# Graph network, layer 2: where x and its constants are added, and how the second norm gets its variance

## The chip, the cores and the metric

The kernel runs on one core of a Trainium2 chip. The metric is the time of one execution on the device in microseconds. A core has five engines with a queue each: TensorE (PE, its weight loads PEld), VectorE (DVE), ScalarE (ACT), GpSimd (POOL) and SyncE (SP). SP only issues DMAs here. GpSimd issues the indirect DMAs (gathers and scatters by a list of row numbers). Sixteen DMA engines carry all of them.

## The reference

A two-layer graph attention network over 10,000 nodes with 768 features and 170,000 edges (self loops included), and a residual norm around it. Cut to what matters:

```python
h = gat_conv(x, edge_index, W1, a_src1, a_dst1, b1, HEADS, HID, True)     # 4 heads of 256
h = relu(layer_norm(h, g1, be1)) + (x @ Wr1 + br1)
h1 = h                                                                   # 1024 columns
h = gat_conv(h, edge_index, W2, a_src2, a_dst2, b2, 1, OUT_DIM, False)   # 1 head of 768
h = layer_norm(h, g2, be2)
h = h + (h1 @ Wr2 + br2)
return _layernorm(x + h)                                                 # no gain, no bias
```

Each `gat_conv` takes, for every node, the softmax over its incoming edges and sums the source nodes' rows by it, and adds its bias. So the end of layer 2 is, for each node: a weighted sum of gathered rows plus b2, a first norm with g2 and be2, the addition of h1 @ Wr2 + br2 and of x, and a second norm. All numbers are float32.

## The kernel before

**Tiles and slots.** Nodes are sorted by their degree and cut into 79 tiles of 128, one node on each partition. A tile of n slots fetches n rows for each of its 128 nodes: slot 0 is the tile's own rows (a plain DMA from SP, L452), the other n - 1 are gathers on GpSimd (L424, one for each slot, 128 rows of 770 numbers). `TURNS` puts the tiles in the order in which both layers work: every other one from small degrees to large, then the rest back. So n runs 8, 10, 11, 12 and so on up to 41 in the middle (tile 39 in this order) and down again to 9; it is 15 to 19 in about half of the tiles, and 1377 in all. Layer 1 (up to about 3428 us) writes each tile's 1024 columns to `h1_d`, its x rows to `x_d` and the rows that layer 2 gathers to `table2`.

**Layer 2** (`ordered_layer2`, L878 on) keeps a ring of 41 slots in SBUF. `ring.fetch(q)` (L449) issues the fetches up to q. The fetch of a slot waits until the slot 41 before it has been read, by VectorE and by TensorE.

For a tile t, in the program's order:

- `residual(t)` (L942), issued a tile ahead on TensorE: into PSUM it sums x (by a product with the identity matrix, L949) and h1 @ Wr2 (L952), 768 columns in two parts.
- `weights_of(t)` (L923), issued inside tile t - 1: its first part, at slot `turn` of that tile (a third of the way, later where the ring is tight), makes the logits of all n slots on VectorE (L477 to L484) and their exponential on ScalarE. It needs all rows of tile t. Its second part, three slots later, makes the weights on VectorE (L496 to L499), on ScalarE a diagonal matrix for each slot (L937), and on TensorE the weighted sum of the last 256 columns (L938), behind the residual in the same PSUM tile.
- The loop over the n slots: VectorE adds each slot's first 512 columns, times its weight, to `acc` in PSUM (`weigh`, L519). Its first addition takes b2 in place of `acc`, so that one reads two tiles in SBUF, ring and b2; the others read one in SBUF and one in PSUM. After each slot, `ring.fetch` goes on by one (L1002). At slot n // 2 the loads of h1 and x for tile t + 2 are issued on SP (`fetch_x`, L903 and L904).
- `norms(t)` (L957), a generator that runs on inside tile t + 1. Step 1, before that tile's first slot: mean and variance of the weighted sum by VectorE's statistics (L577, L579), Ln and Exp on ScalarE (L581, L582). Step 2, at slot 3: `scaled` (L591 twice, L593: times g2 and the deviation, plus be2, which also holds br2 and the share of br1), the addition of the PSUM residual (L962), and mean and variance of the result (L577 twice, L579, then L581 and L582 again). Step 3, at slot 6: minus mean times deviation (L966, VectorE) and the output on ScalarE (L968). Step 4, at slot 9: the scatter to `out` on GpSimd (L970).

Each engine takes its instructions in the program's order, which is written by hand. Two addresses matter: x of the first two tiles is loaded into the end of the ring, for later tiles into parts of the space of W2, which layer 2 doesn't need any more.

The lines that set the order:

```python
if k in (turn, turn + LEAD):            # LEAD is 3
    ready += itertools.islice(ahead, 1)  # weights_of(t + 1)
if k in (LEAD, 2 * LEAD, 3 * LEAD):
    next(last, None)                     # norms(t - 1), steps 2, 3, 4
weigh(acc, ring.slot(FIRST[t] + k), e[:, k], ON_PE2, None if k else b2_b)
ring.fetch(FIRST[t] + k + 1 + ring.size)
if t + 2 < NT and k == n // 2:
    ins[t + 2] = fetch_x(t + 2)
```

Of the kernel before, what the change touches and what calls it, by code (L numbers as in the profile page):

```python
# [28 lines left out]
F32 = mybir.dt.float32  # L29
# [6 lines left out]
P = 128  # L36
# [43 lines left out]
def gnn_kernel(ctx, tc, x, x_cols, src, dst, src_col, dst_col, W1, a_src1, a_dst1, b1, g1, be1, Wr1, br1,  # L80
# [492 lines left out]
    def deviation(small, parts):  # L573

        st = small.tile([P, len(parts), 6], F32, name="st")
        for j, a in enumerate(parts):
            nc.vector.bn_stats(st[:, j, :], a)  # L577
        mv = small.tile([P, 2], F32, name="mv")
        nc.vector.bn_aggr(mv, st.rearrange("p k s -> p (k s)"))  # L579
        sd = small.tile([P, 1], F32, name="sd")  # L580
        nc.scalar.activation(sd, mv[:, 1:2], AF.Ln, bias=eps)  # L581
        nc.scalar.activation(sd, sd, AF.Exp, scale=-0.5)  # L582
        return mv[:, 0:1], sd
# [294 lines left out]
    def ordered_layer2():  # L878
        nonlocal ps_big
        with tc.tile_pool(name="b2", bufs=1) as pool, tc.tile_pool(name="small2", bufs=2) as small, \  # L880
# [17 lines left out]
            firsts = [(at_end(C1), at_end(D0)) for _ in range(min(2, NT))][::-1]  # L898

            def fetch_x(t):  # L900

                hT, xt = firsts[t] if t < 2 else (parts[t % 2], parts[2 + t % 2][:, :D0])
                nc.sync.dma_start(hT, h1_d[t])  # L903
                nc.sync.dma_start(xt, x_d[t])  # L904
                return hT.rearrange("p (k n) -> p k n", n=P), xt

            ins = {0: fetch_x(0)}
            ring.fetch(SLOTS[0])
            adds = [spread(pool, shift, "out", nc.sync)]
            b2_b = spread(pool, b2, "b2", nc.sync)  # L910
            ins[1] = fetch_x(1)
            g2_b, be2_b = (spread(pool, v, n, nc.sync) for v, n in ((g2, "g2"), (be2, "be2")))
            nc.vector.tensor_add(b2_b, b2_b, adds[0][:, :C2])
            adds.append(spread(pool, br2, "out", nc.sync))
            assert SLOTS[0] <= rest // R2 and NT > 1

            ones = pool.tile([1, P], F32, name="ones")
# [24 lines left out]
            def residual(t):  # L942


                hT, xt = ins.pop(t)
                r = ps_big.tile([P, 2 * BANK], F32, name="big")
                for c in range(0, C2, BANK):
                    d = min(C2, c + BANK)
                    nc.tensor.matmul(r[:, c:d], ident, xt[:, c:d], start=True, stop=False,  # L949
                                     skip_group_check=True)  # L950
                    for j in range(K1):
                        nc.tensor.matmul(r[:, c:d], hT[:, j, :], wr2[:, j, c:d], start=False,  # L952
                                         stop=(j == K1 - 1 and d < C2),
                                         skip_group_check=True)
                return r

            def norms(t, h, r, means):  # L957

                stats = deviation(small, [a for m in means for a in pieces(m, C2 - ON_PE2)])
                yield  # L960
                scaled(h, means, stats, g2_b, be2_b)
                nc.vector.tensor_add(h, h, r[:, :C2])  # L962
                mean, inv = deviation(small, pieces(h, C2 // 2))
                yield
                less = small.tile([P, 1], F32, name="less")
                nc.vector.scalar_tensor_tensor(less, mean, -1.0, inv, op0=OP.mult, op1=OP.mult)  # L966
                o = pool.tile([P, C2], F32, name="out")
                nc.scalar.activation(o, h, AF.Identity, bias=less, scale=inv)  # L968
                yield
                nc.gpsimd.indirect_dma_start(  # L970
                    out=out, out_offset=bass.IndirectOffsetOnAxis(ap=nodes(t), axis=0),
                    in_=o, in_offset=None, bounds_check=N - 1, oob_is_err=False)
# [7 lines left out]
            for t in range(NT):  # L980
# [15 lines left out]
                for k in range(n):  # L996
                    if k in (turn, turn + LEAD):
                        ready += itertools.islice(ahead, 1)
                    if k in (LEAD, 2 * LEAD, 3 * LEAD):
                        next(last, None)  # L1000
                    weigh(acc, ring.slot(FIRST[t] + k), e[:, k], ON_PE2, None if k else b2_b)
                    ring.fetch(FIRST[t] + k + 1 + ring.size)  # L1002
                    if t + 2 < NT and k == n // 2:
                        ins[t + 2] = fetch_x(t + 2)
                ready += ahead
                for _ in last:
                    pass
# [2 lines left out]
                    nc.vector.tensor_add(be2_b, be2_b, q[:, :C2])  # L1010
                last = norms(t, h, rs[t], [acc, rs[t][:, C2:2 * C2 - ON_PE2]])
                if t + 2 < NT and t + 2 not in ins:
                    ins[t + 2] = fetch_x(t + 2)
            for _ in last:
                pass

# [269 lines left out]
```

## Time and profile before

| | us |
|---|---|
| median of 6 runs | 5322.07 (5316.48 to 5326.01) |
| the profiled execution | 5326.81 |
| its span | 5325.0 |
| busy in the span: PE, DVE, POOL, ACT | 4762.9, 4284.2, 3230.5, 2798.2 |
| layer 2: its first gather, its last gather, its last scatter | 3428.30, 5255.52, 5312.86 |

The profile's second part cuts the span into 40 slices of 133 us, with the busy share in tenths. Layer 2 is the last 14 or so:

```profile
PE   8999997999999986678999999999998866889998
DVE  5884244899999888788899999589988766789998
ACT  3433443677777776677887777333333222233332
POOL 3445455555666655656666655277777656777774
PEclk9999998999999988889999999999998887889999
DMA  4333625899999998799999999599999989999995
```

A reader should keep in mind that shares are means over a slice, that matmuls are pipelined and their ends modelled, and that instructions which only issue a DMA from SP or wait are not counted as busy. In a timeline, a row is: start, length, engine, line, operation, what it writes and reads, how many are merged, and in brackets the idle time before it with what ended that. In a table of groups, the columns are the count, the busy us with the mean ns of one, and the idle us before them.

### The profile page before, as it was taken

How to read it: one execution, taken by the hardware profiler on the slowest of the kernel's cores; microseconds unless marked ns; L12 is line 12 of the kernel's file. 1: busy time of each engine (PE TensorE's matmuls, PEld its weight loads, DVE VectorE, ACT ScalarE, POOL GpSimd, SP SyncE). 2: the span in 40 equal slices, each digit the busy share in tenths (PEclk: the TensorE clock that was granted, in tenths of full speed). 3: DMA queues.
4: the chain of work that ended last, by engine and by line, in shares of the span. 5: the costliest groups of instructions: out<-in, count | busy, mean ns of one | idle time of the engine just before them, and what ended most of it. 6: DMA issues, size and time to landing. Idle time of an engine off the chain costs nothing. (4 is left out here: it accounts for less than half of the span.)

```text
span 5325.0 us, 59568 instructions
## 1 busy us (share of the span) xinstructions
PE 4762.9 (89%) x15191; PEld 2860.2 (54%) x15191; DVE 4284.2 (80%) x7729; ACT 2798.2 (53%) x8184; POOL 3230.5 (61%) x3159
## 2 busy tenths in 40 slices
PE   8999997999999986678999999999998866889998
PEld 3444443555555554445555555566666544566665
DVE  5884244899999888788899999589988766789998
ACT  3433443677777776677887777333333222233332
POOL 3445455555666655656666655277777656777774
PEclk9999998999999988889999999999998887889999
DMA  4333625899999998799999999599999989999995
GB/s 157 123 100 87 97 87 188 317 335 346 354 368 362 366 332 298 270 330 346 359 365 364 351 333 334 186 381 377 379 366 347 327 275 321 331 352 371 367 384 219
DMA packets 474306, 1591.37 MB, mean 299 GB/s; under 512 B 118327, under 2 KB 122487, under 8 KB 473958
## 3 DMA queue, kind: packets, MB, share of 16 engines
q0 software_dynamic: 322384, 1286.62, 66.2%
q1 hardware_dynamic: 149520, 297.43, 16.2%
q10 hardware_dynamic: 2054, 3.42, 0.2%
q8 instruction: 128, 2.10, 0.2%
q14 instruction: 220, 1.80, 0.1%
HBM read 1431.80 MB, written 177.29 MB: 302 GB/s over the span
## 5 line engine op out<-in xcount | busy, mean ns | idle before, releaser
L424 POOL DMA_INDIRECT ring<-table,slots x2675 | 2649.9, 991 | 1498.4 <-DVE acc L519 373.8
L519 DVE SCALAR_TENSOR_TENSOR acc<-ring,e,acc 128x512 f32<-128x512 f32 (+1 forms) x2530 | 1578.2, 624 | 123.1 <-PE acc L733 47.5
L508 ACT ACTIVATE ring<-ring,e 128x256 f32<-128x256 f32 x3284 | 1337.7, 508 | 0.0
L515 DVE TENSOR_TENSOR acc<-acc,ring 128x1024 f32<-128x1024 f32 x801 | 985.6, 1230 | 79.8 <-ACT ring L508 11.0
L938 PE MATMUL big<-ring,diagonals 128*128 128x256 f32 x2754 | 684.6, 411 | 196.1 <-ACT diagonals L937 186.3
L171 PE MATMUL big<-w,xT 128*128 128x512 f32 x1896 | 827.7, 599 | 22.5 <-DMA w<-in_W_dram 9.9
L826 PE MATMUL half<-w,hT 128*128 128x512 f32 (+1 forms) x2528 | 830.5, 486 | 0.0
L171 PE MATMUL big<-wr,xT 128*128 128x512 f32 x1896 | 830.1, 595 | 0.2 <-ACT xT L706 0.2
L952 PE MATMUL big<-wr,w 128*128 128x512 f32 (+1 forms) x2464 | 822.8, 487 | 0.0
L938 PEld LDWEIGHTS big<-ring,diagonals 128*128 128x128 f32 x2754 | 564.2, 207 | 313.7 <-ACT diagonals L937 217.0
L826 PEld LDWEIGHTS half<-w,hT 128*128 128x128 f32 x2528 | 478.9, 189 | 371.2 <-issue 308.9
L733 PE MATMUL acc<-ring,diagonals 128*128 128x256 f32 x1912 | 481.2, 410 | 193.4 <-ACT diagonals L727 193.0
L952 PEld LDWEIGHTS big<-wr,w 128*128 128x128 f32 x2464 | 470.6, 191 | 327.8 <-issue 296.6
L171 PEld LDWEIGHTS big<-w,xT 128*128 128x128 f32 x1896 | 364.0, 193 | 482.2 <-issue 464.5
L171 PEld LDWEIGHTS big<-wr,xT 128*128 128x128 f32 x1896 | 356.5, 191 | 417.4 <-issue 416.7
L733 PEld LDWEIGHTS acc<-ring,diagonals 128*128 128x128 f32 x1912 | 389.5, 207 | 278.0 <-ACT diagonals L727 217.3
L581 ACT ACTIVATE sd<-mv,eps 128x1 f32<-128x1 f32 x237 | 69.6, 294 | 814.2 <-DVE mv L579 814.2
L937 ACT ACTIVATE diagonals<-ident,e 128x128 f32<-128x128 f32 x1377 | 410.9, 387 | 140.6 <-DVE e L499 131.6
L665 DVE TENSOR_TENSOR scr<-big,ad_b 128x1024 f32<-128x1024 f32 x79 | 96.7, 1224 | 377.9 <-ACT row L662 377.9
L727 ACT ACTIVATE diagonals<-ident,e 128x128 f32<-128x128 f32 x956 | 293.0, 388 | 204.0 <-DVE e L499 203.9
L485 ACT ACTIVATE e<-e 128x68 f32<-128x68 f32 (+29 forms) x160 | 38.2, 239 | 635.9 <-DVE e L484 635.9
L670 POOL TENSOR_TENSOR row<-row,none 128x1024 f32<-128x1024 f32 x79 | 187.1, 2368 | 264.5 <-ACT row L662 264.0
(173 smaller groups left out, 3617.4 us busy)
## 6 DMA issues: line engine op xcount, KB each, us to landing
ring<-table,slots POOLq DMA_INDIRECT x2675, 7.0
table<-row SPq DMA_DIRECT2D x79, 516.0 KB, 3.6
h_d<-hT SPq DMA_DIRECT2D x79, 512.0 KB, 6.5
w<-h_d SPq DMA_DIRECT2D x77, 512.0 KB, 8.3
table<-row SPq DMA_DIRECT2D x79, 385.0 KB, 6.0
ring<-table SPq DMA_DIRECT2D x79, 385.0 KB, 6.5
xT<-in_x_cols_dram SPq DMA_DIRECT2D x79, 384.0 KB, 4.5
x_d<-xt SPq DMA_DIRECT2D x79, 384.0 KB, 6.6
```

The costliest lines, as they stand in the source:

```text
L171: nc.tensor.matmul(p[:, c:e], aT[:, j, :], w[:, j, c:e], start=(j == 0), stop=(j == k - 1))
L424: nc.gpsimd.indirect_dma_start(out=to, out_offset=None, in_=table, in_offset=bass.IndirectOffsetOnAxis(ap=index, axis=0), **more)
L508: nc.scalar.activation(row[:, s], row[:, s], AF.Copy, scale=e[:, h:h + 1])
L515: nc.vector.tensor_add(acc[:, :c], acc[:, :c], row[:, :c])
L519: nc.vector.scalar_tensor_tensor(acc[:, s], row[:, s], e[:, h:h + 1], (acc if first is None else first)[:, s], op0=OP.mult, op1=OP.add)
L670: nc.gpsimd.tensor_add(row[:, :C1], row[:, :C1], b1_b)
L727: nc.scalar.activation(diagonals[:, k * H1 + i, :], ident, AF.Copy, scale=e[:, k, i:i + 1])
L733: nc.tensor.matmul(acc[:, c:d], diagonals[:, k * H1 + i, :], ring.slot(q + k)[:, c:d], start=(k == 0 and c % BANK == 0), stop=(k == m - 1 ...
L826: nc.tensor.matmul(q, hT[:, j, :], w2[:, j, c:c + q.shape[1]], start=(j == 0), stop=(j == K1 - 1))
L937: nc.scalar.activation(diagonals[:, k % G, :], ident, AF.Copy, scale=e[:, k, :])
L938: nc.tensor.matmul(to, diagonals[:, k % G, :], ring.slot(FIRST[t] + k)[:, ON_PE2:C2], start=False, stop=(k == n - 1), skip_group_check=True)
L952: nc.tensor.matmul(r[:, c:d], hT[:, j, :], wr2[:, j, c:d], start=False, stop=(j == K1 - 1 and d < C2), skip_group_check=True)
```

## The change

It touches layer 2 only.

- x is no longer summed by TensorE. `residual` starts with the h1 product. x is loaded into two fixed places (`xs`, in W2's space) by a load of its own.
- In step 1 of `norms`, after the statistics, VectorE adds `be2_b` to x in place. In step 2, `scaled` adds this sum where it added `be2_b`.
- The addition of the PSUM residual becomes a form that also gives the sum of each row (`total`). VectorE's statistics of the result (L577 twice, L579) and L966 go.
- In step 3, ScalarE makes minus the mean from that sum, squares the centred row with the sum of squares as a second output (the squares land in `o` and are overwritten), takes Ln and Exp for the deviation, and makes the output.
- The load of x for tile t + 2 is issued after step 2 of `norms(t)`, so inside tile t + 1 at slot 3; h1's stays at slot n // 2 of tile t. At the start of the layer, x of tiles 0 and 1 is loaded after the first ring rows and constants, and no longer into the ring.

```diff
+            firsts = [at_end(C1) for _ in range(min(2, NT))][::-1]
+            xs = [parts[2 + i][:, :D0] for i in range(2)]
+
+            def fetch_h(t):
+
+                hT = firsts[t] if t < 2 else parts[t % 2]
+                nc.sync.dma_start(hT, h1_d[t])
+                return hT.rearrange("p (k n) -> p k n", n=P)
 
             def fetch_x(t):
-
-                hT, xt = firsts[t] if t < 2 else (parts[t % 2], parts[2 + t % 2][:, :D0])
-                nc.sync.dma_start(hT, h1_d[t])
-                nc.sync.dma_start(xt, x_d[t])
-                return hT.rearrange("p (k n) -> p k n", n=P), xt
-
-            ins = {0: fetch_x(0)}
+                nc.sync.dma_start(xs[t % 2], x_d[t])
+
+            ins = {0: fetch_h(0)}
             ring.fetch(SLOTS[0])
             adds = [spread(pool, shift, "out", nc.sync)]
             b2_b = spread(pool, b2, "b2", nc.sync)
-            ins[1] = fetch_x(1)
+            ins[1] = fetch_h(1)
+            fetch_x(0)
             g2_b, be2_b = (spread(pool, v, n, nc.sync) for v, n in ((g2, "g2"), (be2, "be2")))
             nc.vector.tensor_add(b2_b, b2_b, adds[0][:, :C2])
             adds.append(spread(pool, br2, "out", nc.sync))
+            if NT > 1:
+                fetch_x(1)
...
             def residual(t):
-                hT, xt = ins.pop(t)
+                hT = ins.pop(t)
...
-                    nc.tensor.matmul(r[:, c:d], ident, xt[:, c:d], start=True, stop=False,
-                                     skip_group_check=True)
                     for j in range(K1):
-                        nc.tensor.matmul(r[:, c:d], hT[:, j, :], wr2[:, j, c:d], start=False,
+                        nc.tensor.matmul(r[:, c:d], hT[:, j, :], wr2[:, j, c:d], start=(j == 0),
...
             def norms(t, h, r, means):
 
                 stats = deviation(small, [a for m in means for a in pieces(m, C2 - ON_PE2)])
+                nc.vector.tensor_add(xs[t % 2], xs[t % 2], be2_b)
                 yield
-                scaled(h, means, stats, g2_b, be2_b)
-                nc.vector.tensor_add(h, h, r[:, :C2])
-                mean, inv = deviation(small, pieces(h, C2 // 2))
+                scaled(h, means, stats, g2_b, xs[t % 2])
+                total = small.tile([P, 1], F32, name="all")
+                nc.vector.scalar_tensor_tensor(h, r[:, :C2], 1.0, h, op0=OP.mult, op1=OP.add, accum_out=total)
+                if t + 2 < NT:
+                    fetch_x(t + 2)
                 yield
+                o = pool.tile([P, C2], F32, name="out")
                 less = small.tile([P, 1], F32, name="less")
-                nc.vector.scalar_tensor_tensor(less, mean, -1.0, inv, op0=OP.mult, op1=OP.mult)
-                o = pool.tile([P, C2], F32, name="out")
-                nc.scalar.activation(o, h, AF.Identity, bias=less, scale=inv)
+                nc.scalar.activation(less, total, AF.Copy, scale=-1.0 / C2)
+                nc.scalar.activation(o, h, AF.Square, bias=less, accum_out=total)
+                nc.scalar.activation(total, total, AF.Ln, bias=eps, scale=1.0 / C2)
+                nc.scalar.activation(total, total, AF.Exp, scale=-0.5)
+                nc.scalar.activation(less, less, AF.Copy, scale=total)
+                nc.scalar.activation(o, h, AF.Identity, bias=less, scale=total)
                 yield
...
                     if t + 2 < NT and k == n // 2:
-                        ins[t + 2] = fetch_x(t + 2)
+                        ins[t + 2] = fetch_h(t + 2)
```

More of the change, by code (lines that the diff above doesn't have):

```diff
@@ L897, in ordered_layer2 @@
             nc.vector.tensor_copy(brT, br1_c[:, :, None].to_broadcast([P, K1, P]))
-            firsts = [(at_end(C1), at_end(D0)) for _ in range(min(2, NT))][::-1]
-            def fetch_x(t):
-                hT, xt = firsts[t] if t < 2 else (parts[t % 2], parts[2 + t % 2][:, :D0])
-                nc.sync.dma_start(hT, h1_d[t])
-                nc.sync.dma_start(xt, x_d[t])
-                return hT.rearrange("p (k n) -> p k n", n=P), xt
-            ins = {0: fetch_x(0)}
+            firsts = [at_end(C1) for _ in range(min(2, NT))][::-1]
[4 more added lines that the diff above has]
+                return hT.rearrange("p (k n) -> p k n", n=P)
+            def fetch_x(t):
+                nc.sync.dma_start(xs[t % 2], x_d[t])
+            ins = {0: fetch_h(0)}
             ring.fetch(SLOTS[0])
@@ L1012, in ordered_layer2 @@
                 if t + 2 < NT and t + 2 not in ins:
-                    ins[t + 2] = fetch_x(t + 2)
+                    ins[t + 2] = fetch_h(t + 2)
             for _ in last:
```

## The prediction

> **What bounds the kernel now.** Layer 2 runs from 3428 us to 5313 us; nothing before it changes. The chain of waits was read first and says nothing here: it holds only the last output scatter. So I took the busy times in four stretches of layer 2 (length; then busy us and instructions of PE, PEld, DVE, ACT, POOL; clock, DMA share, GB/s):
>
> ```profile
> 3440.00:4050.00 610.00, 589.89 (x2081) 397.33 (x2080) 537.61 (x1106) 200.47 (x635) 456.01 (x472) 0.98 0.99 374
> 4050.00:4750.00 700.00, 532.06 (x1808) 374.30 (x1807) 520.09 (x983) 195.24 (x626) 473.08 (x496) 0.85 0.90 320
> 4750.00:5256.00 506.00, 487.69 (x1716) 329.40 (x1716) 471.14 (x958) 169.03 (x537) 384.08 (x397) 0.98 0.99 373
> 5256.00:5313.00 57.00, 44.81 (x163) 30.07 (x161) 52.25 (x107) 18.59 (x54) 4.58 (x6) 0.92 0.21 81
> ```
>
> GpSimd looks idle for a quarter of the time, but its timeline has a fixed 0.30 us between two gathers. With that, 456.0 + 472 x 0.30 = 598 of 610 us in the first stretch, 622 of 700 in the second, 503 of 506 in the third. So **issuing gathers sets the pace**: 0.95 + 0.30 = 1.25 us each, and 1298 x 1.25 + 79 x 1.32 (scatters) = 1727 of layer 2's 1885 us. VectorE takes 0.79 n + 7.1 us for a tile of n slots (spacing of its L962 from tile to tile: 16.5 us at n = 12, 18.9 at 15, 20.6 at 17); GpSimd 1.25 n + 0.07. They cross near n = 15, so VectorE is slower only in small tiles.
>
> The groups of layer 2 that matter:
>
> ```profile
> L424 POOL DMA_INDIRECT ring<-table,slots x1298 | 1246.2, 960 | 545.2 <-DVE acc L519 123.3 <-issue 108.1 <-PE big L938 93.9
> L577 DVE BATCH_NORM_STATS2 st<-w 128x6 f32<-128x384 f32 x158 | 80.6, 552 | 2.7
> L593 DVE SCALAR_TENSOR_TENSOR w<-w,sd,be 128x768 f32<-128x768 f32 x79 | 80.4, 1018 | 20.1 <-ACT sd L582 12.1
> L949 PE MATMUL big<-w,ident 128*128 128x512 f32 x154 | 79.8, 600 | 10.3 <-DMA w<-x_d 9.0 <-DVE acc L519 1.2
> L962 DVE TENSOR_TENSOR w<-w,big 128x768 f32<-128x768 f32 x79 | 75.3, 954 | 2.7
> ```
>
> A gather costs 0.960 us in the mean and 0.945 at rest. The timelines of both engines show where the rest goes:
>
> ```profile
> 3634.73 0.95 POOL L424 DMA_INDIRECT ring<-table,slots  x1 [0.30 <-DVE acc L519]
> 3635.98 1.70 POOL L424 DMA_INDIRECT ring<-table,slots  x1 [0.30 <-DVE w L591]
> 3637.98 0.95 POOL L424 DMA_INDIRECT ring<-table,slots  x1 [0.30 <-DVE w L962]
> ...
> 3635.84 1.02 DVE L593 SCALAR_TENSOR_TENSOR w<-w,sd,be 128x768 f32<-128x768 f32 x1
> 3636.89 0.95 DVE L962 TENSOR_TENSOR w<-w,big 128x768 f32<-128x768 f32 x1
> ```
>
> The gather that starts 0.14 us into L593 ends 0.82 us after it: it stood still until L593 was done. L593 reads two SBUF tiles; so does each tile's first L519 (ring and b2). All 37 gathers of layer 2 longer than 1.05 us lie on one of these two; none lies on L962 or L591, which read PSUM and SBUF. A start between 0.1 and 0.9 us into L593 costs 0.89 us less its offset. L593 hits 16 of 79 times, 0.66 us each: 0.134 us a tile.
>
> In the middle stretch (n of 20 and more) GpSimd stops once a tile:
>
> ```profile
> 4169.59 0.94 POOL L424 DMA_INDIRECT ring<-table,slots  x1 [0.30 <-issue]
> 4174.06 0.94 POOL L424 DMA_INDIRECT ring<-table,slots  x1 [3.53 <-DVE acc L519]
> ...
> 4165.32 0.15 DVE L928 TENSOR_TENSOR ad<-ring,lift 128x1 f32<-128x1 f32 x1
> 4171.81 0.19 DVE L477 TENSOR_TENSOR e<-ring,ad 128x22 f32<-128x22 f32 x1 [6.35 <-DMA ring<-table,slots]
> ```
>
> The ring is full, VectorE waits at the logits for the next tile's last gather to land, and only its next L519 frees a slot. These stops sum to 50 us, and two more around the 41-slot tile to 27. VectorE's norms lie inside its own 6 us wait and aren't in this loop.
>
> **The change, part by part.**
>
> *TensorE* loses L949, 0.86 + 0.43 us a tile (from its starts to L952's next), 102 us in all. I credit nothing: it waits for diagonals in the middle, and in the end stretch VectorE reads its sums 5 to 12 us after they are made (last: made 5300.8, read 5305.5). Were it the bound in the ten last tiles, this would be worth 13 us.
>
> *VectorE.* From start to next start, step 2 loses L962 0.99, two L577 1.05 and L579 0.13; L966 is 0 to 0.13. It gains the sum with accumulator, not in this trace in that form: 1.05 as L593, plus 0.04 to 0.12 from L239, whose accumulating operation of 1.68 us repeats every 1.72. Step 1 gains a 768-wide addition of two SBUF tiles: 0.95 (L647), 0.87 if it overlaps the next one as L579 does, at most 0.98. Net -0.34 to -0.02; I take -0.21. It counts only where VectorE runs back to back and behind the data, the last 18 tiles from 4969 us: **-3.8 us**.
>
> *ScalarE* gets copy, square, Ln, Exp, copy, Identity in one piece: 0.20 + 1.03 + 0.10 + 0.29 + 0.20 + 0.20 + 1.03 = 3.1 us in place of 1.03, ahead of the diagonals in its queue, and the square now waits for the previous scatter's landing where L968 did (45 us in 11 places). The cover is TensorE, still in the residual (diagonals at 5239.1, used at 5244.7). Without it TensorE's sums come 2.1 us later, against its 5 us of slack. The scatter behind Identity, in GpSimd's queue, starts no later: from L962 to Identity's end pass 5.6 us today (4159.37 to 4164.95), and 1.1 + 3.1 then, some 1.2 more where the next tile's Exp comes between; a late one would hold the gathers behind it by as much. Behind the last tile there is no cover: addition 0.95 earlier, and 3.33 from the sum to Identity where 3.04 passed from L962 to L968: **+1.2**.
>
> *GpSimd's port.* The new addition reads two SBUF tiles and stands just before the first L519. The trace has no such row; bounds: below, L593's 0.134 scaled to 0.95 us, 0.125 a tile; above, the gather is held through the first L519 too, some 0.6. With starts spread evenly over 1.25 us, 0.72/1.25 = 58% are held, 0.36 us in the mean: 0.21. A held gather ends 0.81 us after the addition, so the third start after it comes 4.56 us after the addition's start, 0.27 us into L593 (4.29 after): 0.62 more in those 58%, less the 0.134 it costs today: +0.28. Nearer to this than to the bottom I take 0.40. It counts in the 61 tiles before VectorE falls behind: **+24.4** (7.6 to 36.6). The Trainium skill (SBUF — State Buffer, "Who interferes with whom") says that a VectorE instruction with two SBUF inputs contends with a GpSimd instruction that reads SBUF, and that the second to issue blocks fully. It speaks against this change, as the row above does. The same section infers that such an addition spares descriptor generation; by that this term would be 0 and the sum 5312, but the 1.70 us row contradicts it.
>
> *SP's queue.* The x load moves from beside h to behind step 2 and waits there for L593's successor; behind it stand h and the next tile's own rows. h is needed a tile later (issued 4157.6, used 4188.4), x two. What moves is the moment: today own rows, h and x (1281 KB) leave together, and gathers issued just after land in 8.5 us, against 4.5 before them. In the ten tiles of 20 and 21 slots h and x now leave some 4 us later, about 1 us ahead of the gather that ends the wait; tiles where all three left that close still show 8 to 9 us. Half a microsecond each: **-5** (-22, all stops of these ten gone; +5, the gather lands later).
>
> *Small.* The 41-slot tile's second stop ends after step 2, shorter by 1.1 (0 to 2). At the start x no longer precedes the first gathers: -1 (0 to -2).
>
> Sum: 24.4 - 5 - 1.1 - 3.8 + 1.2 - 1 = **+14.7 us**. The profiled run took 5326.8 us (span 5325.0), 4.7 above the median of 5322.1; on the median this gives **5337 us**.
>
> **Rivals.** (A) *Faster: the loads leave the ring's way.* With own rows alone ahead, the last gather of the ten tiles lands 2.5 us sooner, all their stops go (-22), and the port costs only its lower bound: 7.6 - 22 - 1.1 - 3.8 + 1.2 - 1 = -19, **5303 us**. For it: 4.5 against 8.5 us. Against: the close-burst tiles. It decides once the landing gains over 1.5 us in these ten. (B) *Hidden anyway:* starts stay locked so that the addition is seldom hit; 7.6 - 5 - 4.7 = -2, **5320**. For it: L593's low count. (C) *Held through both operations:* 36.6 and no gain from the loads, **5354**. For it: gathers of 2.1 to 2.4 us in layer 1 on runs of such operations.
>
> **Numbers.** Forecast 48%, A 24%, B 15%, C 13%. About 0.2% (10.6 us) can be told from no change. Slower by more: 0.8 of the forecast and all of C, 0.51; faster: nearly all of A, some of B, 0.25; within: 0.24. The forecast's own range is 5328 to 5350; with the rivals, 5300 to 5358.
>
> **What would show it.** Gathers over 1.05 us on the new addition and oftener on L593; L424's mean rising from 960 to about 980 ns; the middle stops unchanged or smaller; the last gather issued after 5255.5 us. If the mean stays at 960 the port step is wrong; if the stops shrink to under 1 us, A holds.

## The result, and the profile after

The changed kernel takes 5336.9 us (median of 20 runs, 5328.3 to 5346.4) against 5323.1 us for the kernel before in the same comparison: a ratio of 1.0027, 95% interval 1.0021 to 1.0033. It is slower by 13.8 us. The forecast was 14.7 us slower. The profiled execution took 5336.5 us (span 5334.7).

Busy times of layer 2 in the same three stretches as before, and in the end stretch, which now ends ten us later (length; busy us and instructions of PE, PEld, DVE, ACT, POOL; clock, DMA share, GB/s):

```profile
3440.00:4050.00 610.00, 544.46 (x1915) 370.51 (x1914) 518.67 (x1033) 237.76 (x745) 464.26 (x462) 0.94 0.98 366
4050.00:4750.00 700.00, 511.19 (x1750) 362.19 (x1750) 521.50 (x953) 229.85 (x720) 489.39 (x501) 0.84 0.92 323
4750.00:5256.00 506.00, 453.23 (x1579) 308.08 (x1578) 452.05 (x886) 197.99 (x621) 387.01 (x388) 0.95 0.98 366
5256.00:5323.00 67.00, 52.01 (x188) 34.78 (x187) 60.31 (x120) 27.93 (x83) 14.86 (x16) 0.91 0.38 141
```

TensorE and VectorE do less in the first stretch, as meant (589.9 to 544.5 us, 537.6 to 518.7). GpSimd is busy longer (456.0 to 464.3 us) and yet issues fewer instructions (472 to 462): each takes longer. In the middle stretch it issues more (496 to 501). The groups of layer 2 (count, busy us with the mean ns of one, idle us before them with its releasers; the first four gathers lie ahead of this window):

```profile
L424 POOL DMA_INDIRECT ring<-table,slots x1294 | 1278.7, 988 | 460.3 <-issue 114.8 <-DVE acc L519 109.9 <-PE big L944 89.1
L981 POOL DMA_INDIRECT out_dram<-out,order x79 | 85.6, 1083 | 71.6 <-ACT sd L581 31.2 <-ACT out L979 9.5 <-POOLq L1245 9.0
L593 DVE SCALAR_TENSOR_TENSOR w<-w,sd 128x768 f32<-128x768 f32 x79 | 80.4, 1018 | 32.2 <-ACT sd L582 24.7 <-DVE w L591 0.5
L968 DVE SCALAR_TENSOR_TENSOR w<-big,w 128x768 f32<-128x768 f32 x79 | 75.6, 957 | 2.7
L975 ACT ACTIVATE out<-w,less 128x768 f32<-128x768 f32 x79 | 73.9, 935 | 107.7 <-DMA out_dram<-out,order 105.9
L964 DVE TENSOR_TENSOR w<-w,be 128x768 f32<-128x768 f32 x79 | 70.7, 895 | 0.0
```

The mean gather rose from 960 to 988 ns and the mean scatter from 1024 to 1083. L593 idles 32.2 us where it idled 20.1, for ScalarE's sd; the square L975 idles 107.7 us, nearly all of it for the landing of the previous scatter, where L968 in that place waited 45.3 us for it.

The timeline shows the hold as the prediction described it (start, length, engine, line; VectorE above, GpSimd below):

```profile
3700.53 0.89 DVE L964 TENSOR_TENSOR w<-w,be 128x768 f32<-128x768 f32 x1
3701.34 0.75 DVE L519 SCALAR_TENSOR_TENSOR acc<-ring,e,b 128x512 f32<-128x512 f32 x1
...
3704.82 1.02 DVE L593 SCALAR_TENSOR_TENSOR w<-w,sd 128x768 f32<-128x768 f32 x1
3705.87 0.96 DVE L968 SCALAR_TENSOR_TENSOR w<-big,w 128x768 f32<-128x768 f32 x1
...
3706.76 0.75 DVE L519 SCALAR_TENSOR_TENSOR acc<-ring,e,acc 128x512 f32<-128x512 f32 x1
```

```profile
3700.86 1.36 POOL L424 DMA_INDIRECT ring<-table,slots  x1 [0.30 <-PE big L944]
3702.53 0.94 POOL L424 DMA_INDIRECT ring<-table,slots  x1 [0.30 <-PE big L944]
3703.78 0.94 POOL L424 DMA_INDIRECT ring<-table,slots  x1 [0.30 <-PE big L944]
3705.03 1.63 POOL L424 DMA_INDIRECT ring<-table,slots  x1 [0.30 <-PE big L944]
```

A gather starts 0.33 us into the new addition and takes 1.36 us; it ends 0.80 us after the addition does (3702.22 against 3701.42). The third start after it, 3705.03, falls 0.21 us into L593 and is held again, 1.63 us. In layer 2, 43 gathers and scatters are held on the addition (19.1 us above what they take undisturbed) and 48 on L593 (29.2 us, before: 16 and 10.6); on the first L519 they are 22 (9.3 us, before 29 and 7.2).

Only a start within the addition, or less than 0.03 us ahead of it, is held. A gather that is already under way when the addition begins runs on beside it:

```profile
3787.14 0.95 POOL L424 DMA_INDIRECT ring<-table,slots  x1 [0.30 <-DMA ring<-table,slots]
...
3787.41 0.90 DVE L964 TENSOR_TENSOR w<-w,be 128x768 f32<-128x768 f32 x1
```

Of the 79 additions, 51 began with a gather or scatter that had started at least 0.05 us earlier, and none of these took even 0.01 us longer than undisturbed. The additions did not wait either: 0.896 us with one under way, 0.895 without.

The time from the first gather to the last scatter of layer 2 can be split without remainder: 1298 gathers and the 74 scatters among them at 0.945 and 1.013 us with 0.30 between (1711.9 us up to the last gather's start), what they take above that (**holds**), idle time above 0.30 (**stops**), and the **tail** from the last gather to the last scatter.

| us | holds | stops | of these the middle tiles | tail | all of layer 2 |
|---|---|---|---|---|---|
| before | 20.6 | 94.7 | 45.6 | 57.3 | 1884.6 |
| after | 61.2 | 72.4 | 31.4 | 54.4 | 1899.9 |
| difference | +40.6 | -22.3 | -14.2 | -2.9 | +15.3 |

The middle tiles are numbers 29 to 37 and 41 to 52 (each from its logits to the next tile's), and their column counts only gaps longer by 0.03 us or more, here and in the expectations below. Each split is that of one profiled execution. These two differ by 9.7 us in all, since layer 2 happened to begin 5.5 us earlier in the profile after (3422.84 against 3428.30); layer 1 is the same code. So 41 us came in by held instructions, and 22 went out again by shorter stops. The experiments ask for the cause of each.

### The profile page after: what moved, and what is told of

Same layout as the page of the kernel before. It is cut to its first block, busy times and chain, and to the rows that moved or that the text cites. A ratio compares the mean times of both kernels' runs of the same rounds, so it can differ in the third digit from the quotient of the medians.

```text
span 5334.7 us, 59136 instructions
## 1 busy us (share of the span) xinstructions
PE 4674.7 (88%) x14875; PEld 2804.3 (53%) x14875; DVE 4256.9 (80%) x7571; ACT 2909.2 (55%) x8500; POOL 3270.1 (61%) x3159
## 5 line engine op out<-in xcount | busy, mean ns | idle before, releaser
L424 POOL DMA_INDIRECT ring<-table,slots x2675 | 2684.7, 1004 | 1475.8 <-DVE acc L519 357.6
L519 DVE SCALAR_TENSOR_TENSOR acc<-ring,e,acc 128x512 f32<-128x512 f32 (+1 forms) x2530 | 1582.0, 625 | 126.8 <-PE acc L733 49.2
L944 PE MATMUL big<-ring,diagonals 128*128 128x256 f32 x2754 | 701.3, 418 | 300.7 <-ACT diagonals L943 265.4
L956 PE MATMUL big<-wr,w 128*128 128x512 f32 (+1 forms) x2464 | 807.3, 486 | 6.5 <-DVE new L481 3.0
L944 PEld LDWEIGHTS big<-ring,diagonals 128*128 128x128 f32 x2754 | 575.3, 212 | 425.4 <-ACT diagonals L943 327.8
L668 ACT ACTIVATE scr<-scr 128x256 f32<-128x256 f32 x632 | 253.5, 402 | 120.3 <-DVE scr L665 120.3
```

Of the source, the lines that this page charges most:

```text
L424: nc.gpsimd.indirect_dma_start(out=to, out_offset=None, in_=table, in_offset=bass.IndirectOffsetOnAxis(ap=index, axis=0), **more)
L519: nc.vector.scalar_tensor_tensor(acc[:, s], row[:, s], e[:, h:h + 1], (acc if first is None else first)[:, s], op0=OP.mult, op1=OP.add)
L668: nc.scalar.activation(m[:, s], m[:, s], AF.Copy, accum_out=row[:, C1 + i * H1 + h:C1 + i * H1 + h + 1])
L944: nc.tensor.matmul(to, diagonals[:, k % G, :], ring.slot(FIRST[t] + k)[:, ON_PE2:C2], start=False, stop=(k == n - 1), skip_group_check=True)
```

## The experiments

Every time below is a median, told as its distance from the kernel before on the same chip; the changed kernel's own distance is +13.8 us. The ratios and their intervals are estimated from all runs together and can differ by up to 0.001 from the quotient of the two medians.

**One more addition, in two forms.** The kernel before, with an addition that nobody uses, at the place where the change has its own. The two kernels differ in one operand only:

```diff
+                nc.vector.tensor_add(spare, g2_b, be2_b)        # first kernel
+                nc.vector.tensor_add(spare, r[:, :C2], be2_b)   # second kernel: r in PSUM
                 yield
                 scaled(h, means, stats, g2_b, be2_b)
```

> The kernel before, with one more 768-wide addition of two SBUF tiles (the norm's two constants, into a spare tile, result unused) where the change has its own, just ahead of the tile's first L519. Port theory: some 40 gathers are held by it for some 19 us and hits of L593 rise from 16 to some 45; excess 50 to 60 us in place of 17.8, time 20 to 45 us above the kernel before. Rival (VectorE time alone): excess stays near 18 us and the time rises by at most 18 x 0.9 = 16 us.

> As the run before it, the same place and width, but the addition reads the residual in PSUM and one SBUF tile (result unused again). Port theory: no gather is held by it; excess 15 to 28 us (the shift of the later gathers against L593 falls away with the holding); time above the kernel before by VectorE's own 0.95 us in the last 18 tiles, 10 to 18 us. Rival: no difference between this run and the one with two SBUF tiles.

Measured: with two SBUF tiles +46.2 us (ratio 1.0084, 1.0070 to 1.0098), with one operand in PSUM +32.5 us (1.0059, 1.0046 to 1.0073). The additions' own group and GpSimd's group in layer 2, first of the kernel with two SBUF tiles:

```profile
L963 DVE TENSOR_TENSOR w<-g,be 128x768 f32<-128x768 f32 x79 | 70.9, 897 | 0.0
```

```profile
L424 POOL DMA_INDIRECT ring<-table,slots x1296 | 1281.1, 989 | 482.5 <-PE big L941 106.6 <-issue 104.4 <-DVE acc L519 102.5
```

then of the kernel with one operand in PSUM:

```profile
L963 DVE TENSOR_TENSOR w<-big,be 128x768 f32<-128x768 f32 x79 | 70.7, 895 | 0.0
```

```profile
L424 POOL DMA_INDIRECT ring<-table,slots x1295 | 1245.6, 962 | 499.2 <-DVE acc L519 120.7 <-issue 103.1 <-PE big L941 91.7
```

The additions take the same time to 2 ns, and one of them lengthens the mean gather by 27 ns. With two SBUF tiles the holds are 59.9 us (39 gathers and scatters on the addition, 50 on L593), with one in PSUM 22.3 (none, and 16, as in the kernel before). Not for want of starts: 38 gathers start 0.1 to 0.75 us into the addition that reads PSUM, and none of them takes more than 0.03 us longer than undisturbed. That settles what holds the gathers: the second SBUF operand, not the addition.

The first run came out just above its 20 to 45 us, and the second, expected at 10 to 18, far above that. As no holds were added there, what is left for its 32.5 us is VectorE's time: the addition takes 0.81 us from its start to the next one's, and 32.5 us would be that in some 40 tiles, not in the last 18 alone. The stops and the tail of its profile agree: +10.0 us in tiles 3 to 28, +10.0 in tiles 61 to 78, +9.4 in the tail. With 0.81 us more a tile VectorE sets the pace in the small tiles at the start too.

**The constants on TensorE.** The changed kernel without VectorE's addition. TensorE adds the constants to the residual (the first two tiles keep the addition, since the constants are not complete yet):

```diff
+                    if t > 1:
+                        nc.tensor.matmul(r[:, c:d], ones, be2_b[0:1, c:d], start=True, stop=False,
+                                         skip_group_check=True)
...
+                if t < 2:
                     nc.vector.tensor_add(xs[t % 2], xs[t % 2], be2_b)
```

> The changed kernel without VectorE's addition of the constants (from tile 2 on): TensorE adds them to the residual by one product with ones for each half. x is still added by VectorE as the first norm's vector, squares stay on ScalarE, x is still fetched behind step 2. Port theory: the excess of gathers over 0.945 us falls from 58.8 to 15 to 25 us. If the stops stay at 31 us (loads theory): 5295 to 5306 us, faster than the kernel before. If they grow back (absorption theory): 5308 to 5318. Rival, that the addition costs by its own 0.9 us of VectorE and not by the port: faster than the changed kernel only by 18 x 0.9 = 16 us or less, with the gathers' excess unchanged.

Measured: -6.5 us (ratio 0.9990, 0.9980 to 0.9999), 20 us under the changed kernel. Holds fell from 61.2 to 24.7 us, as the port theory says, and the middle stops stayed small, at 27.8. The time is still not the 5295 to 5306 us that this would give: the tail grew from 54.4 to 63.0 us. Two groups of VectorE from 5000 us to the end of this kernel show what took over:

```profile
L593 DVE SCALAR_TENSOR_TENSOR w<-w,sd 128x768 f32<-128x768 f32 x17 | 17.3, 1019 | 13.9 <-ACT sd L582 13.0
...
L577 DVE BATCH_NORM_STATS2 st<-big 128x6 f32<-128x256 f32 x17 | 7.1, 418 | 11.9 <-PE big L944 11.9
```

In the last tiles VectorE now waits 13.0 us for ScalarE's sd and 11.9 us for TensorE's sums. The second wait is new: L577 on these sums idles neither in the changed kernel nor in the kernel before. TensorE is busy 293.1 of the 300 us from 5000 to 5300 here, 27.2 of them with the constants' products, and idles only 3.2 us for ScalarE's diagonals (281.2 and 13.2 in the changed kernel), so its own work is what makes the sums late, as far as the profile tells. The wait for sd is in the changed kernel already; in the kernel before L593 idled 1.9 us there:

```profile
L593 DVE SCALAR_TENSOR_TENSOR w<-w,sd 128x768 f32<-128x768 f32 x18 | 18.3, 1018 | 8.8 <-ACT sd L582 7.7
```

ScalarE's timeline in the changed kernel has the reason:

```profile
5173.43 0.19 ACT L974 ACTIVATE less<-all 128x1 f32<-128x1 f32 x1
5181.65 0.93 ACT L975 ACTIVATE out<-w,less 128x768 f32<-128x768 f32 x1 [8.03 <-DMA out_dram<-out,order]
...
5183.60 1.03 ACT L979 ACTIVATE out<-w,less,all 128x768 f32<-128x768 f32 x1
5184.54 4.18 ACT L943 ACTIVATE diagonals<-ident,e 128x128 f32<-128x128 f32 x14
5188.62 0.28 ACT L581 ACTIVATE sd<-mv,eps 128x1 f32<-128x1 f32 x1
5188.94 0.20 ACT L582 ACTIVATE sd<-sd 128x1 f32<-128x1 f32 x1
```

The square writes into o, and o is free only when the previous tile's scatter has landed; that scatter was issued at 5173.40, so the square stands for 8.0 us. Behind it in ScalarE's queue are the norm's other operations, the next tile's 14 diagonals and then sd, which L593 needs: it starts at 5189.17, 1.8 us late. Squares into a tile other than o would let the square, Ln and Exp run during that wait, but Identity writes o as well and would still stand for the landing, so a second o would be needed too. Neither was tried.

**x back beside h.** The changed kernel with three x buffers (x's indices become t % 3), meant to let x of tile t+2 leave in the middle of tile t again:

```diff
-            xs = [parts[2 + i][:, :D0] for i in range(2)]
+            space = w2.rearrange("p k n -> p (k n)")[:, 2 * C1:6 * C1]
+            xs = pieces(space[:, :3 * D0], D0)
+            hs = pieces(space[:, 3 * D0:3 * D0 + 2 * C2], C2)
...
-                if t + 2 < NT:
-                    fetch_x(t + 2)
                 yield
...
                         ins[t + 2] = fetch_h(t + 2)
+                        fetch_x(t + 2)
```

> The changed kernel with one part undone: three x buffers, and x of tile t+2 is again fetched beside h in the middle of tile t, as before the change. Loads theory (the stops of the middle tiles shrank from 45.6 to 31.4 us because x left in another moment): the stops come back to 42 to 48 us and the time rises by 8 to 14 us, to 5345 to 5351. Absorption theory (part of the added delay of the gathers falls into stops that would have been waited out anyway): stops 28 to 35 us, time within 4 us of the changed kernel.

Measured: +25.3 us (ratio 1.0047, 1.0034 to 1.0061), 11.5 more than the changed kernel. Holds hardly differ (62.7 against 61.2), stops rise from 72.4 to 83.9, the middle ones from 31.4 to 38.5. So the new order of the loads is worth some 11.5 us (3 to 19 with the two intervals taken together).

It is not the moment of x alone, though. In 13 of the 21 middle tiles, all ten of 20 and 21 slots among them, x leaves at the same moment in both kernels, 17.8 or 18.6 us after the tile's logits (L484), directly behind an L593. Only h goes back there, from 18.2 to 19.0 us to 10.0 to 16.9. In the other 8 x leaves 0.4 us behind h again, 2.6 to 7.3 us later than in the changed kernel.

The stops do not come back to 45.6. In all kernels profiled on chips of this speed the middle stops are 27.8 to 32.6 us where x is issued behind step 2 (four kernels), and 38.5 to 45.6 where it is issued beside h (four kernels), so the order of the loads makes half of the 14.2 us or more. What makes the rest, up to 7 us, stays open. The kernel with the PSUM addition has 40.1 without added holds, so it is not the holds alone; that x still leaves late in those 13 tiles (10.6 to 16.5 us after the logits in the kernel before) is a candidate that was not tested.

The view of DMA issues, for 3440 to 5200 us, has rows on h and x (count, KB, median us from issue to landing), of the kernel before:

```profile
w<-h_d SPq DMA_DIRECT2D x73, 512.0 KB, 8.3
...
w<-x_d SPq DMA_DIRECT2D x73, 384.0 KB, 10.8
```

of the changed one:

```profile
w<-h_d SPq DMA_DIRECT2D x72, 512.0 KB, 8.9
...
w<-x_d SPq DMA_DIRECT2D x71, 384.0 KB, 5.8
```

and of the one with x back (h is at 8.3 us there):

```profile
w<-x_d SPq DMA_DIRECT2D x71, 384.0 KB, 7.9
```

In the changed kernel x lands in about half the time, but it isn't sent apart from h: in those 13 tiles it leaves 0.4 us ahead of h. In the kernel before it left 0.4 to 1.0 us behind h in all middle tiles.

**The addition half a tile earlier.** The changed kernel, with the addition moved to the middle slot of its tile:

```diff
                 stats = deviation(small, [a for m in means for a in pieces(m, C2 - ON_PE2)])
-                nc.vector.tensor_add(xs[t % 2], xs[t % 2], be2_b)
+                if not t:
+                    nc.vector.tensor_add(xs[t % 2], xs[t % 2], be2_b)
...
+                    if t and k == n // 2:
+                        nc.vector.tensor_add(xs[t % 2], xs[t % 2], be2_b)
```

> The changed kernel with the addition of the constants moved from just before the tile's first L519 to the middle slot of the tile itself, half a tile earlier; nothing else moved. Phase theory (a gather held by the addition shifts the third next one into L593): L593's hits fall from 48 to 14 to 28 while the addition itself still holds 30 to 48 gathers; excess 30 to 45 us, time 5318 to 5332. Rival (each operation with two SBUF inputs is hit for itself, wherever it stands, and L593's more frequent hits have another cause): L593 hit 40 times or more, time within 5 us of the changed kernel.

> The changed kernel with the addition of the constants moved to the middle slot of its tile, once more. On a chip that runs the kernel before in some 5323 us: phase theory 5318 to 5332 with L593 hit 14 to 30 times (48 in the changed kernel); rival 5333 to 5341 with 40 hits or more. On a chip with slower transfers the ratio to the kernel before shows only that of the first run of this kernel, 0.986, and the hits.

The first of these runs was on a chip that takes 5616 us for the kernel before (see the end); what can be compared there is the count of holds, 27 on L593 where the run with x alone had 47 on the same chip. On a chip that takes 5324 us, the second measured +3.2 us (ratio 1.0005, 0.9996 to 1.0014), 10.6 under the changed kernel. Holds are 49.3 us instead of 61.2, and they fell in one place: the addition itself still holds 53 gathers and scatters (22.0 us), L593 holds 29 (16.5 us) instead of 48 (29.2 us). The phase argument can be counted directly. In the changed kernel 42 gathers and scatters are held on the addition by more than 0.12 us, and in 33 of these cases the third next one is held on L593, at a median offset of 0.22 us. With the unused two-SBUF addition at the same place it is 37 of 38. With the addition moved it is none of 46.

**One half of the change alone.** Squares without the move of x (the kernel before, with the lines of the change from the accumulating sum to Identity), and the move of x without the squares (the changed kernel, with the kernel before's addition, statistics and Identity):

> The kernel before with the squares alone: accumulating sum and ScalarE's squares in place of VectorE's statistics; x and its constants as before (x by TensorE, constants in the norm's last operation, x fetched beside h). If the work on ScalarE lies behind cover: VectorE saves some 1.1 us a tile where it is behind, 18 to 26 tiles, so 12 to 25 us faster than the kernel before, gathers' excess 15 to 25 us (no new operation with two SBUF inputs). Rival: ScalarE's longer piece holds TensorE's diagonals, and the time stays within 5 us of the kernel before.

> The kernel before with the squares alone, once more, on a chip that runs the kernel before in some 5323 us: VectorE's saving of some 1.1 us in each of 18 to 26 tiles makes it 12 to 25 us faster than the kernel before; rival: ScalarE's longer piece ahead of the diagonals gives it back, within 5 us.

> The changed kernel with the squares undone: x and constants by VectorE, x fetched behind step 2, second norm by VectorE's statistics as before. If the squares bring 1.1 us a tile where VectorE is behind: 16 to 28 us slower than the changed kernel, 5353 to 5365, excess of gathers 50 to 62 us as there. Rival: the squares bring nothing and the time is that of the changed kernel within 5 us.

All three runs fell on chips that take 5612 to 5616 us for the kernel before. Squares alone: ratios 0.9959 (0.9946 to 0.9973) and 0.9979 (0.9966 to 0.9993), that is 20 and 15 us faster by the medians, inside 12 to 25, which was worked out for a faster chip, though; x alone: 0.9924 (0.9909 to 0.9939). Their holds are as expected on any chip: 22.7 and 25.8 us with the squares alone (nothing new reads two SBUF tiles), 55.0 with x alone, with 47 hits on L593 as against 48 in the changed kernel. GpSimd stops for 296 to 370 us in these three profiles, where it is 72 to 111 on the faster chips, so the squares' worth on a faster chip was not measured by itself.

**x's load moved in the kernel before.** The load goes behind step 2 and TensorE keeps its work. Here the products for tile t+2 are issued ahead of that fetch, so they read the x that is in the buffer, that of tile t, and the fetch waits for them:

```diff
                 nc.sync.dma_start(hT, h1_d[t])
-                nc.sync.dma_start(xt, x_d[t])
+                if t < 2:
+                    nc.sync.dma_start(xt, x_d[t])
...
                 nc.vector.tensor_add(h, h, r[:, :C2])
+                if t + 2 < NT:
+                    nc.sync.dma_start(parts[2 + t % 2][:, :D0], x_d[t + 2])
```

> The kernel before with one thing moved: x of tile t+2 is fetched behind step 2 of the second norm, as the change does, and no longer beside h in the middle of the tile; TensorE still adds it. Loads theory (from the run with x back beside h, which was 12 us slower than the changed kernel): the stops of the middle tiles fall from 45.6 to 28 to 36 us, and the time falls by 8 to 14 us against the kernel before, more on a chip whose transfers are slower. Absorption theory: stops 40 us or more, time within 4 us of the kernel before.

Measured, on a chip that takes 5612 us for the kernel before: ratio 0.9999 (0.9987 to 1.0011), nothing gained. In the middle tiles the fetch left anywhere from 2 to 34 us after the tile's logits, with x alone on another such chip 15 to 31 and in the changed kernel 15 to 19. So the moment that was to be tested is not in this run, and it decides nothing about the load.

**No norm operation with two SBUF inputs.** Constants by TensorE as above; x goes into the residual in PSUM, and the norm's last operation adds that:

```diff
-                nc.vector.tensor_add(xs[t % 2], xs[t % 2], be2_b)
+                nc.vector.tensor_add(r[:, :C2], r[:, :C2], xs[t % 2])
                 yield
...
-                scaled(h, means, stats, g2_b, xs[t % 2])
+                mean, inv = stats
+                c = 0
+                for a in means:
+                    d = c + a.shape[1]
+                    nc.vector.scalar_tensor_tensor(h[:, c:d], a, mean, g2_b[:, c:d], op0=OP.subtract, op1=OP.mult)
+                    c = d
                 total = small.tile([P, 1], F32, name="all")
-                nc.vector.scalar_tensor_tensor(h, r[:, :C2], 1.0, h, op0=OP.mult, op1=OP.add, accum_out=total)
+                nc.vector.scalar_tensor_tensor(h, h, inv, r[:, :C2], op0=OP.mult, op1=OP.add, accum_out=total)
```

> Constants by TensorE, and x is added by VectorE into the residual in PSUM in step 1 (one PSUM, one SBUF input); L593's place is taken by an operation that reads the normed vector in SBUF and that residual in PSUM, and accumulates the sum. So no operation of the norms reads two SBUF tiles, only the tile's first L519 does (ring and b2). x is fetched at the tile's start. Port theory: no gather is held on the norms' operations, excess 5 to 12 us; against the run with constants by TensorE and L593 as it was (5317.6 us, excess 22) 4 to 10 us faster where GpSimd sets the pace, 5307 to 5314. Rival: the slow tiles, where VectorE sets the pace, absorb it, and the time stays within 3 us.

> As the run without a two-SBUF operation in the norms (constants by TensorE, x added by VectorE into the residual in PSUM, the last operation of the norm reads that and accumulates the sum), but x is fetched behind step 2 as in the change, not at the tile's start. Port theory: excess of gathers 5 to 12 us, none held on the norms. On a chip that runs the kernel before in some 5323 us: 5303 to 5314 (ratio 0.9965 to 0.9985), a few us under the run with constants by TensorE and L593 as it was (0.9990). On a chip with slower transfers (before at some 5610): x fetched late brings 30 to 50 us, ratio 0.984 to 0.992 where the run with x fetched at the tile's start had 0.9955; if the moment of the fetch does not matter, 0.994 to 0.997.

With x fetched at the tile's start, on a chip at 5616 us: ratio 0.9955 (0.9942 to 0.9969), 12.6 us of holds, none on the norms from the third tile on. With x fetched late, on a chip at 5324 us: **-11.7 us, 5312.7 us, ratio 0.9978 (0.9969 to 0.9987)**, faster than both kernels, with 17.4 us of holds (5 to 12 expected) and none on the norms from the third tile on. Its GpSimd groups:

```profile
L424 POOL DMA_INDIRECT ring<-table,slots x1292 | 1238.3, 958 | 468.6 <-DVE acc L519 106.3 <-issue 102.9 <-PE big L944 96.2
L991 POOL DMA_INDIRECT out_dram<-out,order x79 | 80.0, 1013 | 79.5 <-ACT out L989 25.3 <-ACT sd L581 18.0 <-POOLq L1255 13.9
```

Gathers are back at 958 ns and scatters at 1013. Against the kernel with constants on TensorE and L593 as it was (0.9980 to 0.9999), the intervals overlap: what the last step adds is not separated from nothing. Its end is late in the same way (tail 61.8 us): from 5000 to 5300 us VectorE waits 9.1 us for sd and 11.9 for TensorE's sums.

All kernels profiled on chips of one speed, in the terms of the split (us; hits are gathers and scatters held on the added operation, L593 and the first L519):

| kernel | from before | holds | hits | stops | middle | tail |
|---|---|---|---|---|---|---|
| before | 0 | 20.6 | -, 16, 29 | 94.7 | 45.6 | 57.3 |
| changed | +13.8 | 61.2 | 43, 48, 22 | 72.4 | 31.4 | 54.4 |
| x back beside h | +25.3 | 62.7 | 42, 52, 20 | 83.9 | 38.5 | 54.2 |
| constants on TensorE | -6.5 | 24.7 | 2, 24, 25 | 76.7 | 27.8 | 63.0 |
| unused addition, two SBUF | +46.2 | 59.9 | 39, 50, 24 | 94.0 | 38.6 | 65.9 |
| unused addition, PSUM | +32.5 | 22.3 | 0, 16, 27 | 111.3 | 40.1 | 66.7 |
| addition mid tile | +3.2 | 49.3 | 53, 29, 27 | 72.0 | 30.3 | 53.7 |
| no two SBUF in norms, x late | -11.7 | 17.4 | 2, 0, 33 | 81.3 | 32.6 | 61.8 |

## Why the prediction was right, term by term

The total was right, 5337 against 5336.9 us, with the mechanism it named. Two of its terms were too small, on opposite sides, and they cancelled: 11.8 us too little for the held instructions, 15.2 too little for the stops. That +14.7 and +13.8 us lie so close is luck.

**What sets the pace.** Right. In the 52 tiles outside the start, the middle and the neighbourhood of the 41-slot tile GpSimd stops for only 6.2 us before and 4.7 after; elsewhere it issues at its own pace. In the split, which closes by its construction, the change is +40.6 - 22.3 - 2.9 = +15.3 us, where the prediction had +14.7.

**GpSimd's port, +24.4 (7.6 to 36.6).** Right in kind, too small. In the 61 tiles that the term counted, holds grew by 36.2 us, 0.59 a tile where 0.40 was taken, at the top of the range. The parts: 58% of additions were to hold a gather, 42 of 79 (53%) did by more than 0.12 us; 0.36 us each, measured 0.46; the third next start 0.27 us into L593, measured 0.22. Its two parts summed to 0.49, and the step that failed was to go down to 0.40 from there, since the lower bound had nothing behind it but L593's own low count. Scatters, which are held like gathers (1024 to 1083 ns), were not counted at all. The Trainium skill's rule (SBUF — State Buffer, "Who interferes with whom"), that a VectorE instruction with two SBUF inputs contends with a GpSimd instruction that reads SBUF and that the later one blocks fully, agrees where the GpSimd instruction starts second: 39 gathers and scatters were held, and none when one input is moved to PSUM. In the other order nothing blocked: 51 additions began with a gather or scatter under way and took no longer. What the same section infers, that such an addition spares descriptor generation, the prediction set aside because of its 1.70 us row. That went too far. The row shows that a gather which starts during the operation is held, so that the term isn't 0; but those under way ran on at their usual length, which fits the inference. It would also fit that a gather needs the shared port only at its start, where it could read its row numbers (`slots`, a tile in SBUF). Which part of a gather waits is not shown by any run.

**SP's loads, -5 (-22 to +5).** Right in sign, too small. The prediction priced only the ten tiles of 20 and 21 slots. There h and x did leave later, by 2.1 to 7.3 us (some 4 predicted), and stops fell by 8.6 us, from 22.4 to 13.8. Stops fell as well in the others of the middle, around the 41-slot tile (by 3.9 us, 1.1 predicted) and at the start (by 2.7, 1 predicted). In all, stops fell by 22.3 us where these three terms had 7.1. By the run with x beside h about half of that (11.5 us) is the order of the loads; some 7 us in the middle are not explained.

**VectorE, -0.21 us a tile.** Its saving is larger: from L593's start to the next L519's it was 3.22 us and is 1.94, and the addition costs 0.81 from start to next start, so 1.28 - 0.81 = 0.47. That is outside the range given (0.02 to 0.34), since two operations are cheaper than their nearest rows: the accumulating sum takes 0.89 us from start to next start (3705.87 to 3706.76 above; 1.09 to 1.17 predicted, as its read of the accumulator lies beside the next operation), and the addition 0.81 (0.87).

**ScalarE, nothing but +1.2 at the end.** This step failed. The cover named for its longer piece was TensorE, and TensorE's sums are indeed not late in the changed kernel; but sd, which L593 waits for, stands behind the diagonals in the same queue. L593 idled 8.8 us in the last 18 tiles instead of 1.9. So of VectorE's 0.47 x 18 = 8.5 us there, 6.9 were lost. Tiles 61 to 78 and the tail came out at 1.1 us slower together, where -2.6 was predicted. Of this, 4.4 us are holds, which the port term did not count there; the rest is -3.3, so VectorE's larger saving and this delay nearly cancelled as well. With the constants on TensorE the wait for sd grows to 13.0 us.

**TensorE, nothing.** Right for this change: VectorE does not wait for TensorE's sums at the end of either kernel. The kernel with constants on TensorE gives it back 140 us of products and is still 20 us faster than the changed one, but there the sums are 11.9 us late in the last tiles, so with a faster VectorE the term would not be nothing.

**Rivals.** A (the loads leave the ring's way) falls: it asked for all 22 us of stops in the ten tiles, and 8.6 went there (that all stops together fell by 22.3 is another sum); nor did the port stay at its lower bound. B (starts locked off the addition) falls with 43 hits, C (held through both operations) with the hold ending 0.80 us after the addition.

## What to carry to other kernels

When indirect DMAs issued by GpSimd set the pace, look at what VectorE reads: in these runs an operation with two SBUF inputs held every gather that started well within it until some 0.8 us after its end, but not one that was already under way, and one of its inputs in PSUM avoided that at the same VectorE time (895 against 897 ns). Count the next such operation too, because a held instruction comes out at a fixed moment and can be carried straight into it. When work goes to an engine with time to spare, list all that stands behind it in that engine's queue, small results first, and check what the moved operation's output buffer must wait for.

## What the runs showed of the hardware

A held gather ends some 0.8 us after the VectorE operation that held it, whenever it started within it; one that started at least 0.05 us before the operation is not held by it. A held gather's successors lose the phase they had, and 37 of 38 were delivered to the same offset of a later operation.

The chips differ more than the kernels. On two of the four that ran the experiments, the kernel before took 5612 and 5616 us, on the other two 5324; layer 2 began at nearly the same time (3421 to 3434 us in the profiles of all kernels), and was slower throughout. The first stretch of the kernel with the addition mid tile on one of them:

```profile
3440.00:4050.00 610.00, 520.23 (x1696) 339.91 (x1696) 463.24 (x926) 214.91 (x659) 407.33 (x414) 0.91 0.92 330
```

GpSimd issued 414 instructions there where the same kernel on a faster chip issued 465, at 330 in place of 367 GB/s, and it stopped in nearly every tile (291 us of stops in the terms of the split, 72.0 on the faster chip). What makes these chips slower was not found. There that kernel was faster than the one before (ratio 0.9864, 0.9846 to 0.9881) where on the others it was not (1.0005). So the sign of such a change can depend on the chip; the changed kernel itself was not run on the slower ones.
